# Attention's division by its sums in 32x32-block transposes of VectorE, with a new table of slots

## The chip, the cores and the metric

The kernel runs on one core of a Trainium2 chip. The metric is the device time of one execution in microseconds (us). The engines are named as in the profile: PE is TensorE, DVE is VectorE, ACT is ScalarE, POOL is GpSimd, SP is SyncE, which issues most DMAs. Each engine works through its own queue in order. All data are fp32.

## What is computed

Four layers, each added to x, for 32 batches of 256 positions and 256 features. What matters here is the first one, attention with 16 heads of 16 dimensions, with an extra "own" key for each query:

```python
score_prev = einsum('bhqd,bhkd->bhqk', q, k[:, :, :l1]) * SCALE      # masked by length
score_self = (q * k[:, :, l1:]).sum(-1, keepdims=True) * SCALE
weights = softmax(concatenate([score_prev, score_self], -1), axis=-1)
attn = einsum('bhqk,bhkd->bhqd', weights[..., :-1], v[:, :, :l1])
attn = attn + weights[..., -1:] * v[:, :, l1:]
x = x + attn @ Wo + bo
```

Then follow a small adapter network with a layer norm over the features, a linear layer with weights picked by subject, and a pooling over positions with its own softmax.

## The kernel before

Work goes by pairs of batches, p = 0 to 15; i is 0 or 1 within a pair, b = 2p + i. Every step is a function (`proj_q`, `own`, `s1`, `av`, `norm`, ...), and a hand-written table, the `at(slot, fn, ...)` calls, puts it into a slot relative to its pair. A pair starts 16 slots (PERIOD) after the one before, so a slot holds steps of three or four pairs at once, for instance the scores of pair p beside the layer norm of pair p-2. Slots are named below modulo 16. Within a slot the steps are emitted by `order` (0 first, 2 if not given), then older pair first. The program fixes the order on each engine; nothing is rescheduled.

Attention of one batch:

- `proj_q`, `proj_k`, `proj_ks` (matmuls in `proj_ps`, L407) make queries and keys, transposed, for half c = 0 or 1 of the heads. ACT spreads q and k out (L418), and DVE writes qc (L432), the packed queries; qc's instruction comes after ACT's two on the same PSUM tile. `proj_ks` gives prod, and `own` from it the own score.
- `s1` (matmuls L501, four of 32 rows at once) makes scores into a PSUM tile "s" of four banks, of which there is one; n = 0 to 3 is (c, q half). DVE reduces it to negated maxima nmx (L508). s1 stands in even slots.
- `maxima` and `max_rows` join nmx with the own score, transpose the negated maxima (nm_ps, L535), copy 16 rows of it with ACT (nmT, L537) and write them with four small DMAs into spare rows of q, so that the next matmuls subtract the maximum by themselves. ACT makes eown, the exponential of the own score.
- `s2` (L568, odd slots) makes the transposed scores into the same PSUM tile; ACT makes e = exp of it (L576). `av` (L586) multiplies e by v, padded to 32 columns per head of which column 16 is the mask, so that it gives the sum of the weights. The result is transposed, in one PSUM tile "av".
- `av` ends with an ACT copy avT (L595) to SBUF; `av_back` transposes it on PE (av_ps, L605), adds the own part vse (L613) and the own weight to the sum z (L614), and after the second half takes the reciprocal (L618) and multiplies (att, L620). `att_T` transposes att on PE again (L261) with an ACT copy (L267), and `out_proj` multiplies by Wo (o_ps, L276) and adds x (L638).
- `self_values` makes the own values (vs_ps, L276) and multiplies them by eown (vse, L551).

Later layers that the steps touch: `x1_T`, `hidden`, `adapted` (y_ps, L681; DVE adds at L690), `norm_stats` (L699, L700 on DVE, then rstd on POOL, L702 and L703), `norm` (two times L712 and L716 per batch, all inputs in SBUF), `x2_T`, `subject` (z_ps), `pool_hidden` (t_ps), `pool_scores` (sc_ps; mb, L763), `pool_softmax` (pnmx, L769; exponentials on ACT, L776), `pr_T`, `pooled` (p_ps). `mask_keys` (L344 to L351) runs on POOL, ten instructions a pair.

[...] four for "s", one for "av", and three for everything else, which `g_tile` hands out in turn. So each such tile waits until the tile three before it has been read.

```python
ps_s = ctx.enter_context(tc.tile_pool(name="ps_s", bufs=1, space=PSUM))
ps_av = ctx.enter_context(tc.tile_pool(name="ps_av", bufs=1, space=PSUM))
ps_g = ctx.enter_context(tc.tile_pool(name="ps_g", bufs=3, space=PSUM))
```

## Time and profile before

| | us |
|---|---|
| median of 3 runs | 1177.48 (1172.47 to 1179.31) |
| the profiled execution | 1173.8 |
| its span, first to last instruction | 1172.0 |

Shares of the chain of work that ended last, by engine: PE 55%, DVE 21%, ACT 10%, waiting for nothing visible 6%, POOL 4%, DMA 2%. The granted TensorE clock is 0.988 on average. The largest groups of instructions:

```profile
L508 DVE TENSOR_REDUCE nmx<-s 128x8 f32<-128x2048 f32 x128 | 292.8, 2287 | 49.9 <-PE s L501 49.9
L576 ACT ACTIVATE e<-s 128x2048 f32<-128x2048 f32 x128 | 240.1, 1876 | 124.0 <-PE s L568 123.9
L501 PE MATMUL s<-k,qc 32*128 32x512 f32 x1024 | 148.8, 651 | 13.4 <-ACT e L576 11.5
L568 PE MATMUL s<-q,k 32*128 32x256 f32 x2048 | 146.6, 400 | 14.9 <-DVE nmx L508 14.7
L586 PE MATMUL av<-e,vpad 128*32 128x256 f32 x2048 | 137.5, 386 | 1.0 <-ACT e L576 1.0
```

A line gives place, engine, operation, output and inputs, count; then busy us and mean ns of one; then the idle time of the engine just before them and what ended most of it. Matmul times overlap each other, so a group of eight records with a mean of 651 ns takes 1.07 us in the chain of waits.

### The profile page before, as it was taken

Reading aid. Unit: us, or ns where it says so; the run is one execution under the profiler, and the core shown is the slowest. Engines: PE = TensorE matmul, PEld = TensorE weight load, DVE = VectorE, ACT = ScalarE, POOL = GpSimd, SP = SyncE. Lnnn points to the kernel's source line nnn. Section 1 sums busy time; section 2 is a strip of 40 time slices with the busy share of each in tenths; the row PEclk is TensorE's granted clock in tenths of the full one; section 3 lists DMA queues with packets and bytes.
Section 4 is the critical chain, followed back from the end, with each engine's and each line's share of the span. In section 5 each row is a group of like instructions: output and inputs, shape, how many; then the busy total and the mean of one; then the engine's idle time right before and its main releaser. Section 6 shows DMA issues by size and latency. Waiting matters only on the chain.

```text
span 1172.0 us, 21433 instructions
## 1 busy us (share of the span) xinstructions
PE 1105.1 (94%) x8424; PEld 659.7 (56%) x8424; DVE 697.0 (59%) x1120; ACT 538.0 (46%) x770; POOL 384.4 (33%) x354
## 2 busy tenths in 40 slices
PE   6988999999999999999999999999999999999985
PEld 3635565555655565565655556555565655556563
DVE  4544475764757576475757647575664657567544
ACT  2053545445354544445454544545355454545441
POOL 2514161340615225061512506142250613312121
PEclk9899999999999999999999999999999999999997
DMA  3311121413112141312214121231412213121311
GB/s 133 99 39 52 56 73 38 123 38 91 63 50 83 37 124 38 80 57 64 86 37 123 39 74 57 60 96 38 123 38 58 67 46 114 38 87 39 87 51 54
DMA packets 57962, 80.60 MB, mean 69 GB/s; under 512 B 6726, under 2 KB 39750, under 8 KB 57862
## 3 DMA queue, kind: packets, MB, share of 16 engines
q1 hardware_dynamic: 56758, 76.93, 22.2%
q10 hardware_dynamic: 864, 1.51, 0.4%
q8 instruction: 67, 1.10, 0.4%
q0 software_dynamic: 240, 0.79, 0.2%
q14 instruction: 33, 0.27, 0.1%
HBM read 68.45 MB, written 9.71 MB: 67 GB/s over the span
## 4 chain that ended last, share of the span: by engine, by line
PE 55%; DVE 21%; ACT 10%; issue 6%; POOL 4%; DMA 2%; SPq 1%; DVEq 0%; ACTq 0%; POOLq 0%
DVE nmx L508 10%; PE s L568 9%; PE s L501 8%; PE av L586 5%; PE p_ps L276 5%; ACT e L576 5%; PE kps L407 5%; PE z_ps L276 4%; PE v_ps L276 3%; PE o_ps L276 3%; PE ksps L407 3%; ACT mb L776 2%; DVE x1b L716 2%; DVE x1c L712 2%; DVE mb L763 2%
## 5 line engine op out<-in xcount | busy, mean ns | idle before, releaser
L508 DVE TENSOR_REDUCE nmx<-s 128x8 f32<-128x2048 f32 x128 | 292.8, 2287 | 49.9 <-PE s L501 49.9
L576 ACT ACTIVATE e<-s 128x2048 f32<-128x2048 f32 x128 | 240.1, 1876 | 124.0 <-PE s L568 123.9
L501 PE MATMUL s<-k,qc 32*128 32x512 f32 x1024 | 148.8, 651 | 13.4 <-ACT e L576 11.5
L568 PE MATMUL s<-q,k 32*128 32x256 f32 x2048 | 146.6, 400 | 14.9 <-DVE nmx L508 14.7
L586 PE MATMUL av<-e,vpad 128*32 128x256 f32 x2048 | 137.5, 386 | 1.0 <-ACT e L576 1.0
L568 PEld LDWEIGHTS s<-q,k 32*128 32x128 f32 x2048 | 92.5, 184 | 56.5 <-DVE nmx L508 26.9
L586 PEld LDWEIGHTS av<-e,vpad 128*32 128x32 f32 x2048 | 53.6, 109 | 118.2 <-issue 93.8
L595 ACT COPY avT<-av 128x512 f32<-128x512 f32 x64 | 37.5, 585 | 158.9 <-PE av L586 158.9
L640 POOL TENSOR_TENSOR x1c<-x,an 128x512 f32<-128x512 f32 x32 | 40.7, 1273 | 206.2 <-DVE x L638 204.3
L702 POOL TENSOR_SCALAR rstd<-mv 128x4 f32<-128x4 f32 x16 | 3.8, 238 | 293.3 <-DVE mv L700 293.3
L359 POOL TENSOR_TENSOR xs<-xs,xconst 128x1024 f32<-128x1024 f32 x16 | 37.7, 2358 | 176.8 <-DMA xs<-in_x 176.8
L733 DVE TENSOR_TENSOR x2b<-z_ps,x2b 128x512 f32<-128x512 f32 x32 | 22.1, 692 | 112.4 <-PE z_ps L276 41.4
L638 DVE TENSOR_TENSOR x<-o_ps,xs 128x512 f32<-128x512 f32 x32 | 22.0, 688 | 97.1 <-PE o_ps L276 97.1
L347 POOL TENSOR_SCALAR first<-pos,len_f,xT 128x256 f32<-128x256 f32 x60 | 76.7, 1286 | 3.1
L501 PEld LDWEIGHTS s<-k,qc 32*128 32x128 f32 x1024 | 40.6, 185 | 60.3 <-ACT e L576 27.6
L447 DVE SCALAR_TENSOR_TENSOR prod<-ksps,bcol,qc 128x512 f32<-128x512 f32 x32 | 23.9, 746 | 72.5 <-PE ksps L407 72.5
L418 ACT ACTIVATE k<-kps,kbias,cols 128x512 f32<-128x512 f32 x64 | 46.2, 773 | 44.2 <-PE kps L407 44.2
L276 PE MATMUL z_ps<-ws,x2T 128*128 128x256 f32 x256 | 64.9, 397 | 0.0
L276 PE MATMUL vs_ps<-wvs,fT 128*128 128x256 f32 x256 | 64.3, 394 | 0.0
L276 PE MATMUL p_ps<-x2b,prT 128*128 128x256 f32 x256 | 63.7, 393 | 0.0
L407 PE MATMUL ksps<-fT,wks 128*128 128x512 f32 x128 | 63.5, 618 | 0.0
L407 PE MATMUL kps<-xT,wks 128*128 128x512 f32 x128 | 63.4, 618 | 0.0
(134 smaller groups left out, 1758.4 us busy)
## 6 DMA issues: line engine op xcount, KB each, us to landing
an<-in_adn SPq DMA_DIRECT2D x32, 384.0 KB
mk<-pool_d SPq DMA_DIRECT2D x32, 257.0 KB
fT<-in_fT SPq DMA_DIRECT2D x16, 512.0 KB
xs<-in_x SPq DMA_DIRECT2D x32, 256.0 KB
ws<-in_swT SPq DMA_DIRECT2D x32, 256.0 KB
out<-x2b SPq DMA_DIRECT2D x32, 256.0 KB
xT<-in_xT SPq DMA_DIRECT2D x15, 512.0 KB
wb<-in_sb SPq DMA_DIRECT2D x32, 128.0 KB
```

The lines of the kernel that those rows point to most:

```text
L276: nc.tensor.matmul(ps[:, q, :n], lhsT=lhsT(c, q), rhs=rhs[:, c, :], start=(c == 0), stop=(c == 1),)
L347: eng.tensor_scalar(first[:, c], pos, len_f[:, b : b + 1], xm[:, c, i, 0:1], ALU.is_ge, ALU.mult,)
L359: nc.gpsimd.tensor_tensor(xs.rearrange("p b q d -> p (b q) d"), xs.rearrange("p b q d -> p (b q) d"), xconst.unsqueeze(1).to_broadcast([P, ...
L407: nc.tensor.matmul(ps, lhsT=w[:, ci, c * P : (c + 1) * P], rhs=T[src, p][:, ci].rearrange("p b s -> p (b s)"), start=(ci == 0), stop=(ci = ...
L418: nc.scalar.activation(dst[:, u, c].rearrange("p b s -> p (b s)"), ps, AF.Identity, bias=bias[:, u, c : c + 1], scale=scale[:, u : u + 1],)
L501: nc.tensor.matmul(ps[:, j], lhsT=T["qc", p][r, c, i, q * P : (q + 1) * P], rhs=T["k", p][r, :, c, i, :], start=True, stop=True,)
L508: nc.vector.tensor_reduce(T["nmx", b][:, q, c].rearrange("p u j -> p j u"), ps, AX.X, ALU.max, negate=True,)
L568: nc.tensor.matmul(ps[:, j, k, :], lhsT=T["k", p][r, u, c, i, k * P : (k + 1) * P], rhs=T["q", p][r, u, c, i, :], start=True, stop=True,)
L576: nc.scalar.activation(e, ps, AF.Exp)
L586: nc.tensor.matmul(ps[j * HB : (j + 1) * HB, u, :], lhsT=v_bufs[b % 3][:, k, c * 8 + u * 4 + j, :], rhs=e[:, j, k, :], start=(k == 0), sto ...
L595: nc.scalar.copy(t_, ps)
L640: nc.gpsimd.tensor_tensor(x1c, x1, bc_q(an[:, 2 * D : 3 * D]), ALU.add)
```

## The change

The attention result is no longer carried to query-major layout and back by PE. Instead DVE transposes it in blocks of 32 x 32, straight from PSUM (bt); in that layout a query's 16 values and its sum stand along the free axis, so that the own part and the division are elementwise. A last block transpose (`att_T`) brings the result to the layout that the output projection needs. The own values (vs) and own weights (eown) are brought to the same block layout by DVE. The products and sums on the values go to POOL. The heads are no longer permuted on the host, and `av` picks its v columns in another order. eown's exponential is written by ACT beside the negated maxima, and rides along in their transpose.

```diff
     def maxima(p, i):
...
-        eown = small.tile([P, 2, H], F32, tag="eown", name=f"eown{b}")
-        nc.scalar.activation(eown, T["own", b], AF.Exp)
+        nc.scalar.activation(
+            nm_.rearrange("p q (j s) -> p q j s", j=4)[:, :, :, DH : DH + 4],
+            ow.rearrange("p q (g j) -> p q j g", j=4),
+            AF.Exp,
+        )
...
     def max_rows(p, i):
...
         nc.scalar.copy(t_, ps[0:H])
+        eown = small.tile([P, S // HB, HB], F32, tag="eown", name=f"eown{b}")
+        nc.vector.transpose(eown.rearrange("p g e -> p (g e)"), ps)
...
     def self_values(p, i):
...
-        vse = work.tile([P, 2, H, DH], F32, tag="vse", name=f"vse{b}")
-        nc.vector.tensor_tensor(
-            vse,
-            ps.rearrange("p q (h e) -> p q h e", e=DH),
-            T["eown", b].unsqueeze(3).to_broadcast([P, 2, H, DH]),
-            ALU.mult,
-        )
+        vs = work.tile([P, 2, S // HB, HB], F32, tag="vs", name=f"vs{b}", bufs=3)
+        nc.vector.transpose(
+            vs.rearrange("p c g e -> p (c g e)"), ps.rearrange("p c s -> p (c s)")
+        )
...
+    def weighted(p, i):
+        b = 2 * p + i
+        for c in range(2):
+            vs, e = own_v(b, c), own_e(b, c)
+            nc.gpsimd.tensor_tensor(
+                vs, vs, e.unsqueeze(3).to_broadcast([P, S // HB, 2, DH]), ALU.mult
+            )
...
     def av(p, i, n):
...
         if u == 1:
-            t_ = work.tile([P, 2, S], F32, tag="avT", name=f"avT{b}_{c}")
-            nc.scalar.copy(t_, ps)
+            bt = work.tile([P, 2, S // HB, HB], F32, tag="bt", name=f"bt{b}_{c}", bufs=1)
+            nc.vector.transpose(
+                bt.rearrange("p u g e -> p (u g e)"), ps.rearrange("p u s -> p (u s)")
+            )
...
-    def av_back(p, i, c):
...
+    def with_own(p, i, c):
+        b = 2 * p + i
+        bt = T.pop(("bt", b)).rearrange("p u g e -> p g u e")
+        e, vs = own_e(b, c), own_v(b, c)
+        z = small.tile([P, S // HB, 2], F32, tag="zs", name=f"zs{b}_{c}")
+        nc.vector.tensor_tensor(z, bt[:, :, :, DH], e, ALU.add)
+        nc.vector.reciprocal(z, z)
+        nc.gpsimd.tensor_tensor(vs, bt[:, :, :, 0:DH], vs, ALU.add)
+        nc.gpsimd.tensor_tensor(
+            vs, vs, z.unsqueeze(3).to_broadcast([P, S // HB, 2, DH]), ALU.mult
+        )
...
     def att_T(p, i):
         b = 2 * p + i
-        T["attT", b] = transposed(b, T.pop(("att", b)), "attT", nc.scalar.copy)
+        t_ = work.tile([P, 2, S], F32, tag="T", name=f"attT{b}", bufs=4)
+        nc.vector.transpose(
+            t_.rearrange("p c s -> p (c s)"),
+            T.pop(("vs", b)).rearrange("p c g e -> p (c g e)"),
+        )
```

The table of slots changes with it (o = 8i):

```diff
-    at(-5, proj_q, 1)
-    at(-3, proj_k, 1)
-    at(0, proj_v, 0)
-    at(1, proj_ks, 0)
+    at(0, proj_ks, 0)
+    at(1, proj_v, 0)
+    at(2, proj_k, 1)
+    at(3, proj_q, 1)
-    at(5, proj_v, 1)
-    at(6, own, 0, order=3)
-    at(7, own, 1)
-    at(10, self_values, 0)
-    at(19, self_values, 1)
+    at(6, proj_v, 1)
+    at(6, own, 0)
+    at(11, own, 1)
...
+        at(8 + i, self_values, i)
-        at(o + 8, max_rows, i, order=1)
-        at(o + 15, av_back, i, 0)
-        at(o + 19, av_back, i, 1)
+        at(o + 9, max_rows, i, order=1)
+        at(o + 11, weighted, i)
+        at(o + 15, with_own, i, 0, order=1)
+        at(o + 19, with_own, i, 1, order=1)
...
-    at(31, x1_T, 1, order=3)
-    at(33, hidden)
-    at(34, adapted)
+    at(30, x1_T, 1, order=3)
+    at(31, hidden, order=3)
+    at(33, adapted)
-    at(35, norm_stats)
-    for i in range(2):
-        at(36 + i, norm, i)
-        at(37 + i, x2_T, i, order=3)
-        at(39 + 2 * i, subject, i)
+    at(34, norm_stats)
+    at(34, norm, 0)
+    at(35, norm, 1)
+    at(35, x2_T, 0, order=3)
+    at(37, x2_T, 1)
+    at(39, subject, 0)
+    at(43, subject, 1)
-    at(40, pool_hidden)
+    at(39, pool_hidden)
-        at(44, pr_T, i, order=3)
+        at(44 + i, pr_T, i, order=3)
```

Slot 34 of one pair is slot 2 of the pair two later, slot 35 its slot 3. In the changed kernel DVE's order around there is: nmx of slot 2, bt, statistics, norm of the first batch, z and its reciprocal, norm of the second batch, qc of the younger pair (half 1), nmx of slot 4.

## The prediction

> **What bounds the kernel now.** I read the page's busy table first, then a busy table cut into single periods, then TensorE's and VectorE's timelines of one period, then the chain of waits over the same stretch.

> The busy table (busy us, share, instructions), and one steady period (window, its length, busy us of PE, its weight loads, DVE, ACT, POOL, granted clock, DMA share, GB/s):

> ```profile
> PE 1105.1 (94%) x8424; PEld 659.7 (56%) x8424; DVE 697.0 (59%) x1120; ACT 538.0 (46%) x770; POOL 384.4 (33%) x354
> ...
> 601.00:670.00 69.00, 67.30 (x522) 40.06 (x521) 42.84 (x66) 33.56 (x49) 23.64 (x22) 1.00 0.24 69
> ```

> In a steady period TensorE is busy 67.3 of 69 us. The others have slack on average, but each queue runs in order, so what counts is where their bursts stand. One pair of batches takes 16 slots; the same s2 group starts at 599.4 and at 668.2, so 68.8 us a period, of which TensorE stands about 1.7 us. The four stalls are these lines of its timeline (start, length, what, and in brackets the idle time before it):

> ```profile
> 603.08 1.14 PE L501 MATMUL s<-k,qc 32*128 32x512 f32 x8 [0.30 <-ACT e L576]
> ...
> 608.67 0.66 PE L261 MATMUL attT_ps<-ident,att 128*128 128x128 f32 x4 [0.66 <-ACT k L418]
> ...
> 633.57 1.15 PE L568 MATMUL s<-q,k 32*128 32x256 f32 x16 [0.35 <-DVE nmx L508]
> ...
> 650.59 1.15 PE L568 MATMUL s<-q,k 32*128 32x256 f32 x16 [0.39 <-DVE nmx L508]
> ```

> VectorE works almost without a gap from 631.2 to 650.5, slots 2 to 6. This stretch carries the prediction; its timeline, cut:

> ```profile
> 631.22 2.29 DVE L508 TENSOR_REDUCE nmx<-s 128x8 f32<-128x2048 f32 x1 [0.35 <-PE s L501]
> ...
> 634.63 0.41 DVE L699 BATCH_NORM_STATS2 st<-x1c 128x6 f32<-128x256 f32 x1
> ...
> 638.92 2.28 DVE L508 TENSOR_REDUCE nmx<-s 128x8 f32<-128x2048 f32 x1
> 641.12 1.30 DVE L712 SCALAR_TENSOR_TENSOR x1c<-x1c,mv,an 128x256 f32<-128x256 f32 x1
> 642.53 0.59 DVE L716 SCALAR_TENSOR_TENSOR x1b<-x1c,rstd,x1b 128x256 f32<-128x256 f32 x1
> ...
> 648.25 2.28 DVE L508 TENSOR_REDUCE nmx<-s 128x8 f32<-128x2048 f32 x1
> ```

> Between two maxima (L508) VectorE does at most some 7 us of other work; the statistics lie in one gap and the eight normalizing instructions in the next. That is just what TensorE's two slots of some 4.3 us each can cover. So TensorE is the bound, and VectorE's burst has nothing to spare.

> [...] No run here has the vector transpose in fp32. [...] L712 takes at least 0.453 and at most 1.571 us, and the 1.30 us one above ran into a 1.27 us GpSimd TENSOR_TENSOR (640.87). [...] qc (L432) waits for ACT's two q instructions on the same bank, 51.3 us in 32 waits.

> **The change, part by part, per pair.**

> *Removed.* Four groups av_ps (L605) and two attT_ps (L261), 0.44 us each in the chain: 6 x 0.44 = 2.64 us of TensorE. ACT loses 4 x 0.59 (avT) and 2 x 0.60 (attT), 3.5 us. VectorE loses, for two batches, 2 x 0.68 + 4 x 0.41 + 4 x 0.16 + 2 x 0.35 + 2 x 0.76 = 5.9 us. self_values swaps its operands at the same number of matmuls: nothing.

> *Added.* VectorE: two eown transposes (0.39), two vs, four bt, two attT (0.66 each; attT's source is SBUF), four sums (0.16) and four reciprocals of 16 (0.25, between the 0.16 of 2 elements and the 0.35 of 32): 7.7 us, so 1.8 net on an engine with 26 us free. GpSimd: twelve TENSOR_TENSORs of 256, 0.72 us each (512 take 1.27 and 1024 take 2.36), 8.6 us on 24. As sums both are hidden. with_own's chain through GpSimd has a slot before att_T, some 4 us against 1.5: hidden too. mask_keys (12.7 us on GpSimd) now stands behind these, with 8 slots until kps_0 needs it: hidden. max_rows one slot later leaves its four row DMAs over a slot until s2; the waits table shows no wait of s2 for them before: nothing. In SP's queue load_T and the parameter loads keep slots, adapter and mask loads too.

> *Moved.* Three places cost, each read from the order of instructions per engine in the changed kernel.

> (a) Slots 2 to 4. proj_q(1) goes to slot 3, norm_stats and norm(0) to slot 2, norm(1) to slot 3. VectorE's queue is then: nmx of slot 2, bt, statistics, norm(0), z, norm(1), qc, nmx of slot 4. The s1 of slot 4 reads that qc, so everything in front of qc is on TensorE's path. From the end of slot 2's s1: nmx 2.31 (chain), bt 0.65, statistics 2.13 (634.63 to 636.76), first L712 0.41, rest of the wait for GpSimd's rstd 1.15 (it ended at 638.29, 1.53 after the statistics, plus a signal), three norm instructions 1.39, z and reciprocal 0.40, norm(1) 1.80, qc 0.75, signal 0.05: 11.0 us. [...] the eight norm instructions cost 3.6 alone (4 x 0.41 + 4 x 0.49) and 5.5 on average now (4 x 0.627 + 4 x 0.741); beside them GpSimd now runs up to five TENSOR_TENSORs (four of 0.72, one of 1.27). I take the same 1.9, bounds 0 and 3.5. Sum 12.9. TensorE has in that time av 1.00, kps 1.92, s2 1.07, qps 1.92, x2T 0.44 = 6.35. Stall 6.6 us (4.7 to 8.2).

> (b) Slots 10 to 12. Now: nmx, pnmx, ACT's mb exponentials, q, e, then s1; from nmx at 663.91 to s1 at 671.96 it is 8.05 us, under which TensorE does 8.3 from s1's end on, and 0.30 shows. After: bt (0.65) stands between nmx and pnmx, and the cover is av 1.00, qps 1.92, s2 1.07, z 1.92, own 0.79 = 6.70, as proj_q(1) and av_back are gone from it. Chain from s1's end 0.35 + 8.05 + 0.65 = 9.05. Stall 2.35 (1.5 to 3.0).

> (c) Slot 1. nm_ps now comes behind an odd slot's s2, so ACT does e (1.89) before nmT (0.36), and eown (0.39) waits for nmT on that bank. v_ps is the third tile after nm_ps in a pool of three, so it waits for eown: 2.8 us with signals, against nm 0.37 + y 1.04. Stall 1.35 (0.9 to 1.75).

> **Sum.** Pairs whose slots meet: (a) 14, (b) 13, (c) 14. -2.64 x 16 = -42; the old stalls -1.7 x 14 = -24, of which I leave 0.6 x 14 = +8 at other places; (a) +92; (b) +31; (c) +19. Together +84. On the profiled execution's 1173.8 us (span 1172.0) that is 1258; the median of the runs is 0.3% above that execution, so I say 1260 us, 7% slower.

> **Rivals.**

> *TensorE's saving comes through.* TensorE is the bound, 42 us of its work goes, and with half of the old stalls the time is 1174 - 42 - 12 = 1120; with some stalls left, about 1140. For it: 94% busy. The one mechanism that it needs: VectorE reaches qc in time. It decides below 2.64 + 1.7 = 4.3 us of new stalls a pair. Against it: [...] (a) alone is 11.0 - 6.35 = 4.7. It holds only if bt is nearly free and rstd comes early.

> *The stalls come, at their lower bounds.* (a) 4.7, (b) 1.5, (c) 0.9, 0.3 elsewhere: 66 + 20 + 13 + 4 - 66 = +37, about 1212.

> *The vector transpose costs twice the estimate[...].* bt adds 0.65 to (a) and to (b), eown 0.4 to (c)[...]: 3.3 x 14 = +46, about 1306. For it: no fp32 vector transpose was seen. Against: VectorE's other PSUM reads of 512 take 0.68 to 0.75.

> That the change does not do what it says is excluded: the order of instructions shows the six transpose groups gone from TensorE.

> **How the numbers follow.** Forecast 0.55 (1235 to 1285), lower-bound case 0.17, upper case 0.14, saving comes through 0.11, a balance within 0.5% 0.03. A change of 0.5% is about what runs of this kernel can tell from none (before spread 1172.5 to 1179.3). The range 1200 to 1310 leaves out the fast case and a little above. Slower 0.86, same 0.03, faster 0.11.

> **What would show it.** Right: the waits table has PE s (s1's line) waiting for DVE qc, some 90 us in all, 14 times; s1 waiting for ACT e in slot 12 about 2 us each; v_ps waiting for eown about 1.3 us each; TensorE busy falls by some 40 us while the span grows, and a period is near 75 us. Wrong: a period near 66 us, no wait for qc, or the eight norm instructions and bt together under 3 us between two maxima. A transpose row far from 0.66 us would move the sum by 1.7 us a pair for each 0.65.

## The result, and the profile after

| | us | ratio to before (95% interval) |
|---|---|---|
| before, median of 4 runs | 1178.4 | |
| changed, median of 4 runs | 1313.1 (1311.8 to 1313.5) | 1.115 (1.111 to 1.118) |
| forecast | 1260, range 1200 to 1310 | 1.07 |

The direction was right. The rise is 135 us where 84 were worked out, and the time lies 3 us above the range.

The busy table of the changed kernel, in the page's columns:

```profile
PE 1136.1 (87%) x8040; PEld 636.2 (49%) x8040; DVE 741.9 (57%) x1184; ACT 480.5 (37%) x674; POOL 503.1 (38%) x546
```

TensorE has 384 matmul records less (8424 to 8040), as it should, and yet is busy 31 us longer. The work of the other engines moved roughly as summed: VectorE +45 us (29 summed), GpSimd +119 (138), ACT -58 (-56). So the six transpose groups are gone, but TensorE's remaining matmuls took longer. The place is seen in its timeline of one period, which now lasts 78.5 us (s1 of slot 14 at 605.22 and at 683.71) against 68.8. Cut to the three waits that the prediction named, and to what follows them (start, length, what, idle before):

```profile
621.59 1.99 PE L279 MATMUL v_ps<-wvs,xT 128*128 128x256 f32 x8 [1.35 <-DVE eown L546]
...
632.44 0.30 PE L264 MATMUL x2T_ps<-ident,x1b 128*128 128x128 f32 x1 [1.89 <-DVE x1b L733]
633.27 0.55 PE L264 MATMUL x2T_ps<-ident,x1b 128*128 128x128 f32 x3 [0.53 <-DVE x1b L733]
636.91 2.09 PE L504 MATMUL s<-k,qc 32*128 32x512 f32 x8 [3.09 <-DVE qc L435]
638.93 1.93 PE L612 MATMUL av<-e,vpad 128*32 128x256 f32 x16
640.79 2.35 PE L410 MATMUL ksps<-fT,wks 128*128 128x512 f32 x4
...
674.22 1.14 PE L504 MATMUL s<-k,qc 32*128 32x512 f32 x8 [2.10 <-ACT e L602]
675.29 1.58 PE L612 MATMUL av<-e,vpad 128*32 128x256 f32 x16
676.80 3.12 PE L410 MATMUL kps<-xT,wks 128*128 128x512 f32 x4
```

(c) costs 1.35 us, (a) 1.89 + 0.53 + 3.09 = 5.51, (b) 2.10. Against 1.35, 6.6 and 2.35 forecast these are close. They make up nearly all of TensorE's idle time in this period, 78.49 - 69.48 = 9.01 us in its busy table (columns as in the prediction):

```profile
605.22:683.71 78.49, 69.48 (x497) 38.60 (x496) 45.84 (x70) 29.86 (x43) 31.43 (x33) 0.93 0.21 61
```

A further wait is hidden inside a group: in slot 9, sc_ps takes 1.45 us where it took 0.70 before, because its second half waits for eown.

What was not forecast stands in the lines after (a) and (b): the same s1 that takes 1.14 us elsewhere takes 2.09, av 1.93 in place of 1.07, kps 3.12 in place of 1.98. The busy table by stretches of that kernel says why (window, length, busy us of PE, weight loads, DVE, ACT, POOL, then the granted clock, DMA share, GB/s):

```profile
637.00:641.00 4.00, 4.00 (x25) 1.23 (x26) 1.93 (x1) 0.00 (x0) 3.81 (x5) 0.50 0.02 4
641.00:642.00 1.00, 1.00 (x2) 0.48 (x3) 0.36 (x1) 0.00 (x0) 1.00 (x1) 0.71 0.00 0
642.00:644.00 2.00, 2.00 (x19) 0.91 (x17) 0.82 (x2) 0.00 (x0) 1.81 (x3) 1.00 0.00 0
```

```profile
674.00:676.00 2.00, 1.78 (x20) 0.82 (x24) 0.78 (x3) 0.17 (x1) 2.00 (x4) 0.93 0.01 4
676.00:679.00 3.00, 3.00 (x13) 1.17 (x4) 2.81 (x6) 0.00 (x0) 1.81 (x1) 0.50 0.02 5
679.00:680.00 1.00, 1.00 (x5) 0.40 (x5) 0.00 (x0) 0.04 (x1) 0.00 (x0) 0.94 0.00 0
```

Around each of the two longer waits TensorE was granted half its clock, from 634.8 to 641.6 and from 675.7 to 679.1. In the chain of waits, s1, av and ksps of slot 4 come to 2.09 + 1.86 + 2.28 us in place of 1.07 + 1.00 + 1.92: 2.24 more. In slot 12, av and kps come to 1.52 + 3.04 in place of 1.00 + 1.92: 1.64 more. That is 3.9 us a pair, and 54 us over some 14 pairs, about the 51 us between 84 and 135. The kernel before has no wait above 0.66 us in the steady period that the prediction shows, and a clock of 1.00 there.

VectorE's chain behind (a), cut. From the end of nmx (L511) on, VectorE is idle only for the 1.24 us until rstd, and qc comes last:

```profile
624.72 2.29 DVE L511 TENSOR_REDUCE nmx<-s 128x8 f32<-128x2048 f32 x1 [2.01 <-PE s L504]
626.93 0.71 DVE L621 STREAM_TRANSPOSE bt<-av 128x512 f32<-128x512 f32 x1
...
631.35 0.94 DVE L733 SCALAR_TENSOR_TENSOR x1b<-x1c,rstd,x1b 128x256 f32<-128x256 f32 x1 [1.24 <-POOL rstd L720]
...
635.46 0.73 DVE L733 SCALAR_TENSOR_TENSOR x1b<-x1c,rstd,x1b 128x256 f32<-128x256 f32 x1
636.12 0.74 DVE L435 TENSOR_SCALAR qc<-qps,bcol 128x512 f32<-128x512 f32 x1
639.07 2.29 DVE L511 TENSOR_REDUCE nmx<-s 128x8 f32<-128x2048 f32 x1 [2.21 <-PE s L504]
```

### The profile page after: what moved, and what is told of

Its sections match the earlier page's. It is cut to its first block, busy times and chain, and to the rows that moved or that the text cites. A ratio compares the mean times of both kernels' runs of the same rounds, so it can differ in the third digit from the quotient of the medians.

```text
span 1311.2 us, 20872 instructions
## 1 busy us (share of the span) xinstructions
PE 1136.1 (87%) x8040; PEld 636.2 (49%) x8040; DVE 741.9 (57%) x1184; ACT 480.5 (37%) x674; POOL 503.1 (38%) x546
## 4 chain that ended last, share of the span: by engine, by line
PE 63%; DVE 16%; ACT 10%; issue 6%; POOL 2%; DMA 1%; SPq 1%; ACTq 0%; DVEq 0%; POOLq 0%
PE s L504 12%; PE av L612 9%; PE s L594 8%; ACT e L602 5%; PE ksps L410 5%; PE v_ps L279 4%; PE p_ps L279 4%; PE o_ps L279 4%; PE kps L410 4%; DVE x1b L733 3%; DVE nmx L511 3%; PE z_ps L279 2%; PE vs_ps L279 2%; ACT mb L793 2%; DVE x1c L729 2%
## 5 line engine op out<-in xcount | busy, mean ns | idle before, releaser
L511 DVE TENSOR_REDUCE nmx<-s 128x8 f32<-128x2048 f32 x128 | 293.5, 2293 | 154.4 <-PE s L504 152.7
L504 PE MATMUL s<-k,qc 32*128 32x512 f32 x1024 | 163.0, 709 | 86.1 <-DVE qc L435 47.0
L612 PE MATMUL av<-e,vpad 128*32 128x256 f32 x2048 | 161.2, 439 | 2.0 <-ACT e L602 2.0
L635 POOL TENSOR_TENSOR vs<-bt,vs 128x256 f32<-128x256 f32 x64 | 46.5, 726 | 244.4 <-DVE bt L621 244.4
L612 PEld LDWEIGHTS av<-e,vpad 128*32 128x32 f32 x2048 | 58.4, 119 | 138.5 <-issue 115.6
L279 PE MATMUL v_ps<-wvs,xT 128*128 128x256 f32 x256 | 63.7, 392 | 18.9 <-DVE eown L546 18.9
L636 POOL TENSOR_TENSOR vs<-vs,zs 128x256 f32<-128x256 f32 x64 | 40.8, 637 | 97.5 <-DVE zs L634 84.4
L410 PE MATMUL kps<-xT,wks 128*128 128x512 f32 x128 | 77.4, 735 | 0.0
L482 ACT ACTIVATE vpad<-v_ps,mcol 128x256 f32<-128x256 f32 x64 | 26.8, 470 | 109.7 <-PE v_ps L279 109.7
L264 PE MATMUL x2T_ps<-ident,x1b 128*128 128x128 f32 x128 | 26.6, 312 | 45.4 <-DVE x1b L733 45.4
L410 PE MATMUL qps<-fT,wqs 128*128 128x512 f32 x128 | 65.2, 632 | 0.0
```

What stands on the lines that cost most here:

```text
L279: nc.tensor.matmul(ps[:, q, :n], lhsT=lhsT(c, q), rhs=rhs[:, c, :], start=(c == 0), stop=(c == 1),)
L410: nc.tensor.matmul(ps, lhsT=w[:, ci, c * P : (c + 1) * P], rhs=T[src, p][:, ci].rearrange("p b s -> p (b s)"), start=(ci == 0), stop=(ci = ...
L504: nc.tensor.matmul(ps[:, j], lhsT=T["qc", p][r, c, i, q * P : (q + 1) * P], rhs=T["k", p][r, :, c, i, :], start=True, stop=True,)
L511: nc.vector.tensor_reduce(T["nmx", b][:, q, c].rearrange("p u j -> p j u"), ps, AX.X, ALU.max, negate=True,)
L612: nc.tensor.matmul(ps[j * HB : (j + 1) * HB, u, :], lhsT=v_bufs[b % 3][:, k, 8 * c + 2 * j + u, :], rhs=e[:, j, k, :], start=(k == 0), sto ...
L635: nc.gpsimd.tensor_tensor(vs, bt[:, :, :, 0:DH], vs, ALU.add)
```

## The experiments

Ten kernels ran, each beside the kernel before on the same chip. Theory A throughout: three places in the slot table make waits, and the half clock follows from the waits.

### Is the half clock made by the waits?

Surplus matmuls fill the waits of TensorE; the chains of data that it waits for stay as they are. `filler` issues n matmuls into columns that are overwritten or not read.

```diff
+    def filler(dst, n):
+        for m in range(n):
+            nc.tensor.matmul(
+                dst, lhsT=wqs[:, m % 2, 0:P], rhs=wqs[:, m % 2, :], start=True, stop=True
+            )
...
+        if name == "x2T" and b % 2 == 0:
+            filler(ps[:, 0, :], 3)
...
+        if i == 0 and n == 2 and p >= 2:
+            filler(ps[:, 0, 0, :], 6)
...
+        if i == 1 and p >= 2:
+            filler(own_g[:, 256:512], 4)
```

> The changed kernel with TensorE's waiting filled: 3 surplus matmuls of 128 x 256 before the x2T transposes of the first batch, 6 before the s1 of slot 4, 4 behind the own scores of slot 11. They are written into PSUM columns that are overwritten or not read. No wait of another engine is taken away. Theory A (the clock is halved because TensorE stood still for some us): the clock stays at 1.00 in the steady stretch, the 2.2 us after slot 4 and the 1.6 us after slot 12 go although TensorE has 6.2 us more work a pair: 3.9 x 14 = 54 us less, about 1259 us. Theory C (the clock is cut for another reason, such as load or heat): with more TensorE work the clock is no better, 1313 us or more.

Measured 1263.0 us (1258.6 to 1268.0), ratio 1.074 (1.070 to 1.079): 50 us less than the changed kernel, with more matmul work on TensorE. Its period is 74.7 us (v_ps at 600.28 and 675.01). Behind the same s1 of slot 4 the clock now holds (busy table, columns as above):

```profile
615.00:620.00 5.00, 4.50 (x37) 1.80 (x40) 3.14 (x3) 0.00 (x0) 4.81 (x5) 1.00 0.00 0
```

From 600 to 678 us of this execution the clock is 1.00 throughout, and its mean over the execution is 0.985 against 0.928 in the changed kernel. Theory C falls. The 50 us are the size of the missing term, and what is left, 1263 us, is close to the 1260 of the sum without the clock.

### The three places one by one

Layer norm back in its old slots (a):

```diff
-    at(34, norm_stats)
-    at(34, norm, 0)
-    at(35, norm, 1)
-    at(35, x2_T, 0, order=3)
-    at(37, x2_T, 1)
+    at(35, norm_stats)
+    at(36, norm, 0)
+    at(37, norm, 1)
+    at(37, x2_T, 0, order=3)
+    at(38, x2_T, 1, order=3)
```

> The changed kernel with one edit: the statistics and both normalizations go back to slots 35, 36 and 37, where they stood before the change (x2_T with them, to 37 and 38). qc of slot 3 then has only nmx, bt, z and the statistics in front of it. Theory A (the place of the layer norm in VectorE's queue makes stall (a), and the half clock after it follows from the stall): the wait of s1 for qc falls from 5.5 us a pair to under 1, the half-clock stretch after it goes, some 1 to 2 us come back as waits for nmx and attT in slots 5 to 7; about 6.5 us x 14 pairs less, 1200 to 1235 us. Theory B (VectorE's and GpSimd's added work as such[...] makes the loss): the same work is still there, so at least 1290 us.

Measured 1262.6 us (1.073, 1.070 to 1.076). 50 us less, about half of what was expected. Both theories missed: the layer norm matters, but s1 still waits for qc. From the timeline of this kernel's TensorE:

```profile
618.14 1.37 PE L504 MATMUL s<-k,qc 32*128 32x512 f32 x8 [2.44 <-DVE qc L435]
```

There are two chains into qc. The second goes through ACT: behind s2 of slot 3 its queue holds k, then e, then q (1.45 + 1.87 + 1.46 us), and qc (0.75) waits for q on the same PSUM tile. The layer norm's chain had hidden it. A half clock still follows both waits in this period: 3.41 us behind this one, where (a)'s lasted 6.83, and behind the 2.09 us wait for e av takes 1.94 us and kps 2.64.

max_rows an even slot earlier (c):

```diff
-        at(o + 9, max_rows, i, order=1)
+        at(o + 8, max_rows, i, order=1)
```

> The changed kernel with one edit: max_rows at o + 8 in place of o + 9, in an even slot, so that ACT copies nmT without an exponential e in front. Theory A (stall (c) is v_ps waiting for the PSUM tile that eown reads last): v_ps no longer waits (1.35 us a pair), nor sc_ps (0.3 to 0.4); about 1290 us. Rival: the wait only moves to the next PSUM tile: 1305 to 1320 us.

Measured 1292.1 us (1.098, 1.093 to 1.103): 21 less, the number that was expected. No idle before v_ps is left in its period, and sc_ps is back at 0.70 us. But that the number came out so is in part luck, for the half clock moved too. The period is about 75 us in the first four pairs and up to 78.5, as in the changed kernel, in most of the later ones, and the mean clock is 0.915 against 0.928. In such a pair the half clock covers the s1 of slot 12 as well:

```profile
660.01 2.09 PE L504 MATMUL s<-k,qc 32*128 32x512 f32 x8 [2.19 <-ACT e L602]
```

The pooling's exponentials behind the attention's (b):

```diff
-    at(42, pool_softmax, (0, 1))
+    at(43, pool_softmax, (0, 1))
```

> The changed kernel with one edit: pool_softmax at slot 43 in place of 42, so that ACT makes q and the next e before the four exponentials of the pooling. Theory A (stall (b) is ACT's queue, and the half clock of some 4 us after it follows from the stall): the 2.1 us wait of s1 for e in slot 12 and the 1.6 us lost to the half clock behind it both go, 3.7 us x 13 pairs = 49 us less, about 1265 us. Rival 1 (the half clock has another cause than the stall): only 27 us less, about 1286 us. Rival 2: the exponentials are late for prT instead: no gain.

Measured 1270.0 us (1.082, 1.077 to 1.086): 43 less, for a wait of 2.1 us in at most some 14 pairs. The wait alone would be 27 to 29; the half clock behind it goes with it, and in the period from 599.45 to 674.39 us only the one at (a) is left (s1 2.09, av 1.94, ksps 2.62). The same s1, av and kps in this kernel's timeline (av and kps took 1.58 and 3.12):

```profile
648.26 1.14 PE L504 MATMUL s<-k,qc 32*128 32x512 f32 x8
649.33 1.07 PE L612 MATMUL av<-e,vpad 128*32 128x256 f32 x16
650.33 1.98 PE L410 MATMUL kps<-xT,wks 128*128 128x512 f32 x4
```

### Was qc the cause of (a), or only its first victim?

```diff
+    at(-5, proj_q, 1)
...
-    at(3, proj_q, 1)
```

> The changed kernel with one edit: proj_q(1) back at slot -5, so that qc is long there at slot 4 and slot 11 has 1.9 us of TensorE work more. If qc alone were the cause of stall (a): all of (a) goes, and (b) by the cover, about 1155 us. My theory: VectorE's queue is the cause and qc only its first victim; TensorE then waits in slot 3 for the normalized x1b that x2T transposes (3.7 us), and a little for nmx; (a) shrinks by only some 0.8 us, its half clock mostly stays, (b) and its half clock go: about 1250 us.

Measured 1263.8 us (1.073, 1.069 to 1.077). "qc alone" would have given 1155. With qc ready long before, TensorE waits for the layer norm itself, as the timeline shows (3.71 us, where 3.7 were expected):

```profile
608.70 0.48 PE L264 MATMUL x2T_ps<-ident,x1b 128*128 128x128 f32 x1 [3.71 <-DVE x1b L733]
```

VectorE's burst is the cause, with the wait for rstd in it; whoever reads from it first waits. The 14 us above the expected 1250 have a likely source in a new wait: proj_q(1), back in slot 11, waits 1.12 us a pair for a qc (L435).

### The slots or the layout?

The kernel before, in its old layout, with the new slot table; the edit is the second diff of the change, with `av_back` in `with_own`'s places and

```diff
-        at(8 + i, self_values, i)
+        at((10, 17)[i], self_values, i)
```

> The kernel before, with its own layout (TensorE transposes, no block transposes) and the new table of slots, av_back in with_own's places; only self_values stays at slots 10 and 17, since its own weights exist only then. Theory A (the slots make the loss): the wait for qc in slot 4 comes with them, 5 to 6 us a pair, and some 2 us of half clock behind it; stall (b) not, since self_values covers it; the old stalls of 1.7 us go: 1250 to 1285 us. Theory B (the layout makes it): 1170 to 1190 us.

Measured 1315.3 us (1.119, 1.115 to 1.123). Theory B is excluded. The size was underrated again: beside 0.44 + 0.53 + 4.06 us of (a), this kernel waits in one period 0.86 for vs_ps, 0.83 for nmx and 1.06 for e. With this table the old layout takes as long as the new one, so the slots alone are enough for a loss of this size. That the two times are equal does not measure the layout's share: the waits differ, and so may the half clock behind them (its period here is 77.9 us, s1 at 600.10 and at 678.01, against 78.5).

The smallest part of it alone, the two projections of half 1 in the kernel before:

```diff
-    at(-5, proj_q, 1)
-    at(-3, proj_k, 1)
+    at(2, proj_k, 1)
+    at(3, proj_q, 1)
```

> The kernel before with one edit: proj_k(1) at slot 2 and proj_q(1) at slot 3, as in the new table; the layer norm and all else stay. Theory A (two chains meet at qc in slot 3, ACT's k, e, q and VectorE's layer norm): only ACT's chain is there, s1 of slot 4 waits some 2.2 us a pair, and half of TensorE's slot 11 is free, so that the wait for e there grows to 2 us; with the half clock behind them about 6 us x 14, 1245 to 1275 us. If qc's place matters only together with the layer norm: within 10 us of the kernel before.

Measured 1248.5 us (1.063, 1.059 to 1.068), within what theory A expected. Its timeline of TensorE has both waits. The half clock follows only some of them: behind the first of these two s1 takes 1.14 us, behind the second 1.62, and the mean clock from 60 to 1090 us is 0.99.

```profile
606.99 1.14 PE L501 MATMUL s<-k,qc 32*128 32x512 f32 x8 [2.32 <-DVE qc L432]
...
642.20 1.62 PE L501 MATMUL s<-k,qc 32*128 32x512 f32 x8 [2.02 <-ACT e L576]
```

Two moved lines cost 72 us: one opens a chain through ACT in slot 3, and both take away the matmuls that covered ACT's chain in slots 10 to 12.

### Repairing the table

All three edits together (layer norm, max_rows, pool_softmax):

> The changed kernel with all three edits together: layer norm back at slots 35 to 37, max_rows at o + 8, pool_softmax at 43. Theory A (the new layout is sound and three slots cost it everything): the sum of the three, about 160 us less than the changed kernel, 1130 to 1165 us, faster than the kernel before. Theory B (the layout itself loads VectorE and GpSimd too much): above 1178 us.

Measured 1193.0 us (1.015, 1.012 to 1.017). 120 us less than the changed kernel, close to the sum of the three alone (50 + 21 + 43 = 114), though each of these has its own share of the clock in it. It is short of what was expected, and the chain through ACT is still there: s1 waits 2.44 us for qc. So proj_q(1) goes back to slot -5 as well, and proj_v(1) fills slot 3:

```diff
+    at(-5, proj_q, 1)
...
-    at(3, proj_q, 1)
...
-    at(6, proj_v, 1)
+    at(3, proj_v, 1)
```

> The three edits together, and two more: proj_q(1) back at slot -5 (slot 11 of the pair before), and proj_v(1) at slot 3 in place of 6, so that slot 3 still has work beside s2. What is to be told apart is the 2.44 us that s1 still waits for qc with the layer norm out of the way: theory A, it is a second chain through ACT in slot 3 (k, e, q, and then qc), hidden before behind the layer norm; then it and the half clock behind it go, 3.6 us x 14 less, about 1145 us, faster than the kernel before. Theory D, VectorE is simply too busy in slots 2 to 6: the waits for x1b (0.5 us) and attT (0.7 us) in slot 5 grow by about as much, 1175 to 1195 us.

Measured 1174.5 us, ratio 0.999 (0.997 to 1.001): no change against before. The wait for qc is gone, but theory D had the better of the number. In slots 4 to 7 TensorE now has several short waits, most of them for VectorE; o_ps is put to ACT's x2T here and to VectorE's attT in other periods.

```profile
638.46 0.33 PE L264 MATMUL x2T_ps<-ident,x1b 128*128 128x128 f32 x1 [0.31 <-DVE x1b L733]
639.38 0.55 PE L264 MATMUL x2T_ps<-ident,x1b 128*128 128x128 f32 x3 [0.59 <-DVE x1b L733]
640.75 1.97 PE L279 MATMUL o_ps<-wos,attT 128*128 128x256 f32 x8 [0.82 <-ACT x2T L270]
...
647.16 1.15 PE L594 MATMUL s<-q,k 32*128 32x256 f32 x16 [0.90 <-DVE nmx L511]
```

Last, the transpose attT in front of the layer norm in VectorE's queue:

```diff
-        at(o + 20, att_T, i, order=3)
+        at(o + 20, att_T, i, order=1)
```

> The kernel of the run before with att_T at order 1, in front of the normalization in VectorE's queue. o_ps then does not wait for attT (0.7 us a pair), x2T waits some 0.7 us more for x1b: within 10 us of the run before. If one of the two waits is hidden by the other: 5 to 10 us less.

Measured 1162.4 us, ratio 0.989 (0.986 to 0.992): 1.1% faster than the kernel before, and 12 us less than the run before, where at most 10 were expected. The profiled execution is the fastest of six (1154.8 us, clock 0.987; the others 1158.1 to 1164.7, clock 0.978 to 0.981). In it the wait of o_ps is gone and the period is 67.4 us (s2 at 599.75 and at 667.13):

```profile
PE 1066.4 (92%) x8040; PEld 611.6 (53%) x8040; DVE 745.3 (65%) x1184; ACT 486.7 (42%) x674; POOL 500.1 (43%) x546
```

Here TensorE's saving shows: 1105 us busy before, 1066 now, with the 39 us near the 42 that the six groups were priced at. The time falls by 14 us only (1176.4 to 1162.4); the waits for VectorE that are left, and the lower clock of the other executions, are where the rest can be.

## Why the prediction was wrong, step by step

**Right.** The bound: TensorE, with VectorE's burst beside it. The removed work, 42 us: 39 in the repaired kernel. (c): 1.35 us forecast and measured. (b): 2.35 forecast, 2.10 measured. (a): the chain from s1's end to the next s1 was priced at 12.9 us and took 12.2 (624.70 to 636.91); the wait 6.6 and 5.5. In it, bt took 0.71 for 0.65, rstd's wait 1.24 for 1.15; the eight norm instructions average 0.536 (L729) and 0.717 (L733), 5.0 us for the 5.5 priced. The 1.9 us in this price is read from the kernel before, where the norm instruction L716 took 0.48 us in the 12 of 64 cases in which no GpSimd instruction overlapped it, and up to 1.50 in the others. The transposes, priced at 0.66 and 0.39 us by the author's estimate, took 0.67 to 0.72 and 0.45; attT from SBUF took 0.70 as well. The rival with transposes at double price is excluded (1.6 of its 3.3 us are the norm instructions of (a) at the upper bound, 3.5 in place of 1.9). SP's queue and the row DMAs: s2 waited 0.9 us in all for q's rows, where nothing was forecast. One detail of (a) was wrong: x2T was counted as 0.44 us of cover, but it reads the layer norm and waits itself, so that the wait stands at two places. The run with qc early shows that VectorE's order is the cause. (c) left out sc_ps of slot 9, which also waits for eown, some 0.7 us.

**The step that failed** is the sum, "(a) +92; (b) +31; (c) +19. Together +84": each wait entered with its length only, and what it does to the clock was put at nothing without a reason. The waits of (a) and (b) also cost the clock of the matmuls after them, 2.24 and 1.64 us a pair, some 54 us in all. The run that fills the waits shows it: 50 us come back while the chains of data stay. The longest single waits at the two places were 3.09 and 2.10 us, and half clock, 0.50, stood around both. The prediction read the clock column (1.00) of the kernel before and did not ask what longer waits would do to it. The range's upper end missed for the same reason: it was drawn for the transposes and the norm instructions, not for this.

**Rivals.** "The saving comes through" is excluded for this table; in the repaired table a third of it does. The lower-bound case is excluded by the waits' sizes.

**Left open.** How much of the last 28 us (42 less 14) goes to which wait in the repaired kernel was not tried. Why the old layout in the new table takes 1315 where 1250 to 1285 were expected is read from its waits, not separated by runs. Nor was it separated how much of each single repair is the wait and how much the clock.

## What to carry to other kernels

Price a wait on TensorE twice: its length, and the matmuls that run at half clock behind it, where the clock falls. In the changed kernel waits of 5.5 us cost 7.8, and one of 2.1 us cost 3.7. In a hand-written slot table look for what stands in an in-order queue between two steps that TensorE needs, and count it against the matmuls of just those slots; in this case the sum over the period showed none of it. And when a wait is removed, look for the second chain into the same instruction before promising the whole of it.

## What the hardware showed that was not expected

A wait of 2.10 us was enough to halve the clock, and the cut came late: in the changed kernel TensorE stopped at 672.1 and resumed at 674.2 at full speed, and the clock fell to 0.50 only at about 675.7, for 3.41 us, in the midst of work. Its 14 waits of 1.35 us before v_ps never brought it. In the kernel before with its two late projections, the 2.32 us wait is followed by s1 in 1.14 us, the shorter wait of 2.02 us by s1 in 1.62.

```profile
601.77:605.19 3.42, 2.89 (x12) 1.46 (x10) 2.50 (x5) 1.48 (x2) 3.08 (x3) 1.00 0.35 143
605.19:608.60 3.41, 1.61 (x20) 0.68 (x24) 1.63 (x3) 0.96 (x2) 3.29 (x3) 1.00 0.00 0
608.60:612.01 3.41, 3.41 (x32) 1.80 (x28) 3.39 (x2) 0.49 (x1) 3.12 (x4) 1.00 0.00 0
...
639.32:642.73 3.41, 1.39 (x16) 0.73 (x12) 2.21 (x5) 2.83 (x3) 1.75 (x1) 1.00 0.00 0
642.73:646.14 3.41, 3.41 (x25) 1.10 (x18) 2.27 (x2) 0.00 (x0) 0.00 (x0) 0.50 0.00 0
```

The wait of 2.32 us lies across a border, 0.53 us in one step and 1.80 in the next, and nothing follows; the wait of 2.02 us lies in one step, and the next runs at half clock. The period of the changed kernel settles on whole steps: between its waits before v_ps it grows from 77.7 us to 78.5, 23 steps, and stays there from the fifth period on. In the kernel with qc early it is 75.1 us, 22 steps (x2T at 608.70 and at 683.78), and with the pooling late 74.9 (s1 at 599.45 and at 674.39). That the clock holds a kernel at whole steps was not shown. All this is read from the traces; no run was made to test it.
